# A fused attention kernel's slot loop: a third place for odd slots' tiles, logits turned group by group, no chunk steps beside tables, weights' products on quarters

## Chip, core and metric

The kernel runs on one core of a Trainium2 chip. The metric is the device time of one execution in microseconds (us). Five engines work side by side[...]: TensorE (PE), VectorE (DVE), ScalarE (ACT), GpSimd (POOL) and SyncE (SP). The last two serve here above all to issue DMA transfers.

## The reference

Everything is in fp32. The input x is 2 images of 512 channels on a 32 x 32 grid. Two layers follow each other.

Layer 0 is deformable attention with 8 heads of 64 channels. Per head, 64 key positions are found from the queries (a depthwise 6 x 6 convolution with stride 4, a gelu, a small product and a tanh), x is sampled there, and keys and values are made from the samples. A bias is added to the logits of every pair of a query (1024) and a key (64), and it is a small network of the pair's offset in position:

```
off  = tanh(gelu(dwconv(q) + b) @ off_pw) * 4             # where the keys lie
kv   = grid_sample(xn, grid + off);  k, v = kw @ kv, vw @ kv
pos  = grid_q[:, None] - grid_kv[None]                    # 1024 x 64 x 2 per head
bias = relu(signlog(pos) @ w1 + b1)                       # 128 wide
bias = relu(bias @ w2 + b2) @ w3 + b3
out  = softmax(q k^T / 8 + bias) v
x    = x + out_w @ out + out_b
x    = x + mlp(bn(x))                                     # 512 -> 2048 -> 512
```

Layer 1 is plain attention over the 1024 positions of each image with 512 channels, with a residual.

## The kernel before

**The slot loop.** 16 groups (image, pair of heads, head) of 64 keys are worked in 256 slots of 4 keys each (`NS = NG * NSL`). For the offset network a group of 16 keys, 4 slots, shares two tables `ta` and `tb` that hold the first layer's part from x and from y. Slot s does the following:

- `st_layer1` (L616): DVE adds the two tables' rows into `h1` (128 x 4096), two slots ahead.
- `st_layer2` (L633): PE multiplies h1 with the second layer's weights, 32 rows of the output at a time on four column parts of the array. The four quarters z = 0 to 3 go one after another through the three PSUM places of the pool `zp` (a tile of 128 x 1024[...]). ACT evicts each with a relu, z = 0 and 2 into tiles `rx` (L642), z = 1 and 3 into others (L644): z = 3 into `ub`, and z = 1 into `ua`, `uo`, `uc`, `uo` for s % 4 = 0 to 3. So `uo` is the tile of the odd slots. It has two places.
- `st_sum` (L652): DVE adds rx into the z = 1 tile and into ub.
- A chain of DMA transfers with addition (L654, L671, issued by POOL) and of plain copies (L678 and L687, issued by SP) folds and joins the tiles of 8 slots in SBUF until few are left. An odd slot's tile is read by a join two slots later.
- `st_layer3` (L719), every eighth slot: PE multiplies what is left with the third layer's weights into the logits `sim`, on top of the product of queries and keys (L702).

In slots with s % 4 = 0, the **table slots**, SP also loads the features for the next table (L585) and ACT makes the next `ta` and `tb` (L596, L604), after the slot's second eviction.

**Chunk steps.** The keys of later groups are made while earlier groups are worked. A generator `later()` first multiplies two weights (tile `psu`, L503), and then, for chains of one or two head pairs, runs the query product (`psq`, L273), the convolution (`prod`, L319 on ACT, reductions L334 on DVE), gelu and tanh, the features that tables are loaded from (`fe`, stored to `fdr`), the sampling (`pkv`, L471), and the products for keys (`pkk`, L485) and values (`pkv`, L487). It is cut in steps by `yield`. Every slot takes one step behind its fourth eviction until the generator is done:

```python
            if bg is not None:
                with tc.issue_after(evicted[s][1]):
                    next(bg, None)
```

**Softmax steps.** When a group's logits are whole, a second generator `softmax_steps` takes a step in slots that are no table slots, behind the second eviction. ACT brings the logits to SBUF (`ss`, L733), PE turns them by transposes into a PSUM tile `pt` of the pool `zp` (L744), ACT copies them to `sx` (L746), and maximum, exponentials, sums and scaling follow (L751 to L766). The two heads of a pair share the softmax: the first one's logits wait in `ss` until the second's are there, and both are turned together.

All PSUM tiles of the chunk and softmax steps come from the same three places of `zp` as the second layer's tiles. The order of instructions on each engine is fixed when the program is built: the source's order, changed by `issue_after`.

**After the loop** come the output projection, the MLP and layer 1, bound by PE products (L903, L956, L1087, L1185).

Of the kernel before, what the change touches and what calls it, by code (L numbers as in the profile page):

```python
# [14 lines left out]
P = 128  # L15
# [31 lines left out]
def conv_seq_kernel(ctx: ExitStack, tc: tile.TileContext, x, xt, kst, pst, cst, vec, wsm, outw, w1, w2, wl, wlt, brow, out):  # L47
# [12 lines left out]
    def col(name, i=0):  # L60
        return vs[:, VOFF[name] + i : VOFF[name] + i + 1]
# [73 lines left out]
    def flat(name):  # L135
        return zp.tile([P, 2, 512], F32, tag="ps2", name=name).rearrange("p h n -> p (h n)")
# [4 lines left out]
    with tc.tile_pool(name="lp", bufs=2) as lp:  # L141
# [273 lines left out]
        def sample(ci):  # L415
            G = CHAINS[ci]
            K = len(G)
            th = state[ci]
            gx = th[:, 0:2].rearrange("p i g j -> p (i g j)")

            nc.vector.tensor_scalar(gx, gx, 1.0, 16.0, ALU.add, ALU.mult)
            if ci > 0:
                yield


            sg = ph.tile([P, 5, 2, K * J], F32, tag="fe", name="sg")
            hat = sg[:, 0:4].rearrange("p a f j -> p (a f j)")[:, 0 : 4 * K * J]
            nc.scalar.activation(hat, gx, AF.Abs, bias=edge[:, 0:1])
            nc.scalar.activation(hat, hat, AF.Relu, bias=edge[:, 1:2])
            nc.scalar.activation(hat, hat, AF.Relu, bias=1.0, scale=-1.0)  # L430
            yield
            nc.vector.tensor_tensor(sg[:, 4], sg[:, 0], sg[:, 1], ALU.mult)
            hx = ph.tile([P, 2, K, J], F32, tag="hx", name="hx")
            hxf = hx.rearrange("p f k j -> p (f k j)")
            nc.scalar.activation(hxf, th[:, 0].rearrange("p g j -> p (g j)"), AF.Abs, bias=hb[:, 0:1])
            nc.scalar.activation(hxf, hxf, AF.Relu, bias=1.0, scale=-1.0)
            yield
            gy = th[:, 1].rearrange("p (f k) j -> p f k j", f=2)
            for i, (b, k) in enumerate(G):
                g = b * NCH + k  # L440
                xnt = ph.tile([P, 8, P], F32, name="xnt")
                nc.sync.dma_start(out=xnt, in_=xt[:, b, k])
                wk = ph.tile([P, P], F32, name="wk")
                nc.sync.dma_start(out=wk, in_=wsm[:, 512 + k * P : 512 + k * P + P])
                wt = ph.tile([P, 8, 2, J], F32, tag="xn", name="wt")
                for t in range(8):
                    if t == 4:
                        yield
                    nc.scalar.activation(wt[:, t], gy[:, :, i, :], AF.Abs, bias=hb[:, 1 + t : 2 + t])
                yield  # L450
                wtf = wt.rearrange("p t f j -> p (t f j)")
                nc.scalar.activation(wtf, wtf, AF.Relu, bias=1.0, scale=-1.0)

                kv, uv = (ph.tile([P, J], F32, name=name) for name in ("kv", "uv"))
                rowwise, natural = "p (e i t) -> p e i t", "p (i e t) -> p e i t"
                for f in range(2):
                    r, v = slice(64 * f, 64 * f + 64), sg[:, 4, f, i * J : (i + 1) * J]
                    nc.scalar.activation(
                        uv[r].rearrange(rowwise, e=2, t=16), v[r].rearrange(natural, e=2, t=16), AF.Copy,
                        scale=col("bn1b", k)[r],  # L460
                    )
                yield
                nc.vector.tensor_tensor(
                    wt, wt, hx[:, :, i, :].unsqueeze(1).to_broadcast([P, 8, 2, J]), ALU.mult
                )
                yield
                ps = flat("pkv")
                for t in range(8):
                    for f in range(2):
                        r = slice(64 * f, 64 * f + 64)  # L470
                        nc.tensor.matmul(  # L471
                            ps[r, 0:J], xnt[:, t, r], wt[:, t, f, :], start=(t == 0), stop=(t == 7)
                        )
                nc.scalar.activation(
                    kv.rearrange(rowwise, e=2, t=16), ps[:, 0:J].rearrange(natural, e=2, t=16), AF.Copy,
                    scale=bns[:, k : k + 1],
                )
                nc.vector.tensor_tensor(kv, kv, uv, ALU.add)
                if i + 1 == K and ci + 1 < len(CHAINS):
                    xn0.append(load(*CHAINS[ci + 1][0]))  # L480
                yield


                ps, pk = flat("pkv"), flat("pkk")
                nc.tensor.matmul(pk[:, 0:J], wk, kv, start=True, stop=True)  # L485
                for f_, h_, f, h in QUADS:
                    nc.tensor.matmul(  # L487
                        ps[h_, f * 512 : f * 512 + 256], kv[f_, :], uo[f_, k, h * 256 : (h + 1) * 256],
                        start=True, stop=True,
                    )  # L490
                nc.scalar.activation(kz[:, g], pk[:, 0:J], AF.Copy, scale=DH ** (-0.5))
                for f_, h_, f, h in QUADS:
                    nc.scalar.copy(vp[f_, g, h * 256 : (h + 1) * 256], ps[h_, f * 512 : f * 512 + 256])
                yield
            state[ci] = None

        def later():

            for k2 in range(2):
                ps = flat("psu")  # L500
                for k in range(2):
                    c = 2 * k2 + k
                    nc.tensor.matmul(  # L503
                        ps[:, 512 * k : 512 * k + 512], wv[:, c * P : (c + 1) * P], ow_s[:, c, :],
                        start=True, stop=True,
                    )
                nc.scalar.copy(uo[:, 2 * k2 : 2 * k2 + 2, :].rearrange("p k o -> p (k o)"), ps)
                yield
            yield from sample(0)
            for ci in range(1, len(CHAINS)):  # L510
                yield from chain(ci)
                yield from sample(ci)
# [60 lines left out]


        NS = NG * NSL
        tabs, h1s, sums, sims, logits, added = {}, {}, {}, {}, {}, {}
        evicted, raw = {}, {}


# [46 lines left out]
        def st_layer2(s):  # L626
            h1 = h1s.pop(s)
            r = []
            for z in range(4):
                ps = zp.tile([P, 2, 512], F32, name="ps2")  # L630
                for h in range(2):
                    for q in range(4):
                        nc.tensor.matmul(  # L633
                            ps[32 * q : 32 * q + 32, h, :], cw2[:, 32 * z : 32 * z + 32],
                            h1[:, 16 * h : 16 * h + 16, q, :], start=True, stop=True,
                        )
                name, bufs = (
                    ("rx", 3), (("ua", 4), ("uo", 2), ("uc", 2), ("uo", 2))[s % 4], ("rx", 3), ("ub", 3)
                )[z]
                o = lp.tile([P, 2, 512], F32, name=name, bufs=bufs)  # L640
                if z % 2 == 0:
                    nc.scalar.activation(o, ps, AF.Relu, bias=sc[:, 4 + z : 5 + z])  # L642
                else:
                    nc.scalar.activation(o, ps, AF.Relu, bias=sc[:, 4 + z : 5 + z], scale=sc[:, z : z + 1])  # L644
                r.append(o)
                if z % 2 == 1:
                    evicted.setdefault(s, []).append(nc.cur_bb.bb.instructions[-1])
            sums[s] = r
# [78 lines left out]
        def softmax_steps(gi):  # L727
            b, k, f = groups[gi]
            sim = sims.pop(gi)
            if f == 0:  # L730
                logits[0] = f_pool.tile([P, 2, 512], F32, name="ss")
            ss = logits[0]
            nc.scalar.activation(ss[:, f], sim, AF.Identity, bias=col("cb3"))  # L733
            yield

            of = [f] if gi >= NG - 2 else [0, 1][: 2 * f]
            if not of:
                return
            n = len(of)
            pt = flat("pt")  # L740
            for i, g in enumerate(of):
                for c in range(4):
                    o = 512 * i + c * P
                    nc.tensor.transpose(pt[:, o : o + P], ss[:, g, c * P : (c + 1) * P], ident)  # L744
            e = sx[:, :, of[0] : of[-1] + 1, :]
            nc.scalar.copy(  # L746
                e.rearrange("p a f j -> p f a j"), pt[:, 0 : 512 * n].rearrange("p (f a j) -> p f a j", f=n, j=J)
            )
            yield
            mx = f_pool.tile([P, 8, 2], F32, name="mx", bufs=2)  # L750
            nc.vector.tensor_reduce(mx[:, :, 0:n], e, AX.X, ALU.max)  # L751
# [36 lines left out]
        for s in range(NS):  # L788
# [18 lines left out]
                with tc.issue_after(evicted[s][0]):  # L807
                    st_tables(s // 4 + 1)
            st_sum(s, 0)
            if bg is not None:  # L810
                with tc.issue_after(evicted[s][1]):
                    next(bg, None)
            if bg is not None and state.get(len(CHAINS) - 1, 0) is None:
# [559 lines left out]
```

## Time and profile before

| | us |
|---|---|
| median of 3 runs | 2662.8 (2661.68 to 2663.64) |
| profiled execution, time | 2660.99 |
| its span, first to last instruction | 2659.2 |
| slot loop, about | 37 to 1906 |
| PE busy | 2633.2 |
| DVE busy | 2241.3 |
| ACT busy | 1687.2 |

The profile is of one execution. A line of its groups gives the source line, the engine, the operation, tiles out<-in, shapes and count, then the busy time and the mean of one in ns, and after the second bar the idle time of the engine just before, with what ended most of it. A line of the timeline gives start and length in us, the engine, the line and the tiles, and in brackets an idle time before it. A line of the waits view says who waited for whom: us in total, times, longest. A line of the windows view gives start and end, the length, and per engine the busy time with the number of its instructions. PEld is the load of weights into the array. One fp32 matmul shows as two records.

### The profile page before, as it was taken

To read this page: it belongs to the slowest core of one execution; us is meant where nothing else is said; L and a number is where in the kernel's file an instruction comes from. 1 tells how busy PE (TensorE), PEld (TensorE's weight loads), DVE (VectorE), ACT (ScalarE), POOL (GpSimd) and SP (SyncE) were. 2 spreads that over 40 slices of the span, in tenths; PEclk is the share of its full clock that TensorE was granted. 3 is DMA by queue.
4 is the path that set the end of the run, shared out by engine and by line. 5 is a ranking of instruction groups with operands and counts; after the bars stand their busy time and mean duration, and the time that the engine had idled before them with its cause. 6 is when DMAs were issued, how large, how long until landed. Compare 5 with 4: busy or idle time off the path is not lost.

```text
span 2659.2 us, 46896 instructions
## 1 busy us (share of the span) xinstructions
PE 2633.2 (99%) x19344; PEld 965.0 (36%) x19344; DVE 2241.3 (84%) x1329; ACT 1687.2 (63%) x2201; POOL 792.3 (30%) x867
## 2 busy tenths in 40 slices
PE   9999999999999999999999999999999999999999
PEld 3332322433333333233323323333334444446454
DVE  7999999999999999999999999999674483466354
ACT  5887898789978888877777777777621131114041
POOL 1333333333333333333333333333343232000000
PEclk9999999999999999999999999999999999999999
DMA  5887878888788887888888888878730111000000
GB/s 187 181 176 169 191 164 171 181 189 180 171 176 174 192 175 172 171 177 176 171 172 183 175 178 178 172 173 181 191 110 33 48 48 48 0 16 0 32 0 32
DMA packets 116293, 366.77 MB, mean 138 GB/s; under 512 B 23376, under 2 KB 27616, under 8 KB 113392
## 3 DMA queue, kind: packets, MB, share of 16 engines
q0 software_dynamic: 69408, 235.31, 46.9%
q1 hardware_dynamic: 46240, 128.15, 13.8%
q8 instruction: 153, 2.51, 0.4%
q14 instruction: 60, 0.49, 0.1%
q10 hardware_dynamic: 432, 0.31, 0.0%
HBM read 74.81 MB, written 6.55 MB: 31 GB/s over the span
## 4 chain that ended last, share of the span: by engine, by line
PE 60%; DMA 25%; DVE 7%; issue 6%; ACT 1%; POOL 1%; SPq 0%; POOLq 0%; DVEq 0%; ACTq 0%
PE ps L633 31%; PE sw L956 14%; PE sw L1087 9%; DMA uc<-uo 7%; DMA uc<-uc 6%; DMA ua<-uc 4%; DMA uc<-ub 4%; DVE h L616 3%; PE sw L1185 2%; DMA ua<-uo 1%; DVE ub L652 1%; PE psg L535 1%; DMA ua<-ua 1%; PE sim L719 1%; DVE uo L652 1%
## 5 line engine op out<-in xcount | busy, mean ns | idle before, releaser
L633 PE MATMUL ps<-h,cw 128*32 128x512 f32 x16384 | 1782.8, 592 | 8.1 <-ACT rx L642 6.1
L616 DVE CUSTOM_DVE_ANT_1 h<-ta,tb 128x4096 f32<-128x4096 f32 (+1 forms) x257 | 1131.0, 4402 | 28.1 <-PE ps L633 24.2
L633 PEld LDWEIGHTS ps<-h,cw 128*32 128x32 f32 x16384 | 554.7, 110 | 1205.0 <-issue 1114.6
L642 ACT ACTIVATE rx<-ps,sc 128x1024 f32<-128x1024 f32 x512 | 568.1, 1110 | 146.3 <-PE ps L633 116.4
L644 ACT ACTIVATE ub<-ps,sc 128x1024 f32<-128x1024 f32 x256 | 308.2, 1204 | 80.5 <-PE ps L633 80.2
L652 DVE SCALAR_TENSOR_TENSOR ub<-rx,sc,ub 128x1024 f32<-128x1024 f32 x256 | 326.8, 1277 | 6.6 <-ACT ub L644 6.6
L671 POOL DMA_DIRECT2D ua<-uc x126 | 158.3, 1272 | 299.5 <-DMA ua<-uc 292.5
L671 POOL DMA_DIRECT2D ua<-ua x189 | 225.4, 1336 | 20.2 <-DMA ua<-uo 16.2
L644 ACT ACTIVATE uo<-ps,sc 128x1024 f32<-128x1024 f32 x128 | 154.2, 1205 | 74.3 <-PE ps L633 46.2
L956 PE MATMUL sw<-xb,w1t 128*128 128x512 f32 x448 | 193.7, 592 | 2.7 <-DVE xs L123 2.7
L956 PE MATMUL sw<-hm,w2t 128*128 128x512 f32 x448 | 193.6, 592 | 0.0
L654 POOL DMA_DIRECT2D uo<-ub x127 | 126.8, 998 | 210.8 <-DVE ub L652 200.1
L652 DVE SCALAR_TENSOR_TENSOR uo<-rx,sc,uo 128x1024 f32<-128x1024 f32 x128 | 163.5, 1278 | 18.9 <-ACT uo L644 18.9
L123 DVE TENSOR_TENSOR hm<-hm,sw 128x1024 f32<-128x1024 f32 x56 | 67.6, 1218 | 104.5 <-PE sw L956 104.3
L671 POOL DMA_DIRECT2D uc<-uo x63 | 54.0, 857 | 340.8 <-DMA uc<-uo 340.4
L956 PEld LDWEIGHTS sw<-xb,w1t 128*128 128x128 f32 x448 | 85.0, 190 | 110.2 <-issue 105.7
L965 ACT ACTIVATE hm<-hm,vs 128x512 f32<-128x512 f32 x64 | 42.6, 713 | 128.4 <-DVE hm L123 128.4
L956 PEld LDWEIGHTS sw<-hm,w2t 128*128 128x128 f32 x448 | 85.1, 190 | 107.1 <-issue 106.2
L123 DVE TENSOR_TENSOR xs<-xs,sw 128x1024 f32<-128x1024 f32 (+1 forms) x48 | 55.6, 1171 | 75.9 <-PE sw L1087 36.0
L654 POOL DMA_DIRECT2D ua<-ub x64 | 59.3, 926 | 178.4 <-DVE ub L652 163.4
L1087 PE MATMUL sw<-aT,vt 128*128 128x512 f32 x224 | 96.7, 593 | 0.3 <-ACT aT L1167 0.3
L596 ACT ACTIVATE ta<-fb,vs 128x512 f32<-128x512 f32 (+1 forms) x65 | 88.5, 1364 | 10.1 <-DMA fb<-fdr 10.1
(247 smaller groups left out, 2191.6 us busy)
## 6 DMA issues: line engine op xcount, KB each, us to landing
uo<-ub POOLq DMA_DIRECT2D x127, 512.0 KB, 5.5
fb<-fdr SPq DMA_DIRECT2D x64, 512.0 KB, 5.2
ua<-ub POOLq DMA_DIRECT2D x64, 512.0 KB, 6.0
uc<-ub POOLq DMA_DIRECT2D x64, 512.0 KB, 5.0
ua<-ua POOLq DMA_DIRECT2D x63, 256.0 KB, 6.3
ua<-uo SPq DMA_DIRECT2D x63, 256.0 KB, 2.5
ua<-uo POOLq DMA_DIRECT2D x63, 256.0 KB, 5.6
uc<-uc POOLq DMA_DIRECT2D x63, 256.0 KB, 7.2
```

The costliest lines, as they stand in the source:

```text
L123: nc.vector.tensor_tensor(out, a, b_, op)
L596: nc.scalar.activation(ta.rearrange("p j x -> p x j")[:, :, j0:j1], fb[:, 0, :, j0:j1], AF.Identity, bias=col("cb1"), scale=col("w1x"),)
L616: nc.vector._custom_dve(TENSOR_ADD_SAT, out=h1[:, y : y + step].rearrange("p y t x -> p (y t x)"), in0=a.unsqueeze(1).to_broadcast([P, ste ...
L633: nc.tensor.matmul(ps[32 * q : 32 * q + 32, h, :], cw2[:, 32 * z : 32 * z + 32], h1[:, 16 * h : 16 * h + 16, q, :], start=True, stop=True,)
L642: nc.scalar.activation(o, ps, AF.Relu, bias=sc[:, 4 + z : 5 + z])
L644: nc.scalar.activation(o, ps, AF.Relu, bias=sc[:, 4 + z : 5 + z], scale=sc[:, z : z + 1])
L652: nc.vector.scalar_tensor_tensor(r[1], r[0], sc[:, z : z + 1], r[1], ALU.mult, ALU.add)
L654: nc.gpsimd.dma_start(out=sums[s][1], in_=sums[s][3], accum_op=ALU.add)
L671: nc.gpsimd.dma_start(out=out, in_=in_, accum_op=ALU.add)
L956: nc.tensor.matmul(ps[:, m, :], w[:, a, k, m * P : (m + 1) * P], x[:, b_, k, :], start=(k == 0), stop=(k == 1),)
L1087: nc.tensor.matmul(ps[:, m, :], w[:, a, k, c + m * P : c + (m + 1) * P], x[b_][:, k, :], start=(k == 0), stop=(k == nk - 1),)
L1185: nc.tensor.matmul(v[:, m, :], xbl[b_][:, k, m * P : (m + 1) * P], gn[:, a, k, :], start=(k == 0), stop=(k == 1),)
```

## The change

Five edits in the loop's generators and pools:

1. `uo` gets three places instead of two. The tile `ss` shrinks to one group's logits.
2. `softmax_steps` turns each group's logits in its own step, four transposes and a copy of 128 x 512, where a pair's eight transposes and one copy of 128 x 1024 stood in the second group's step. The last two groups were turned singly before already.
3. From slot 60 on, table slots take no chunk step.
4. The key product shares the PSUM tile of the value products (`pkk` goes into columns 256 to 319 of `pkv`).
5. The two weights' product, four matmuls of 128 x 128 by 512 in two tiles, is done on its diagonal blocks alone, as sixteen matmuls of 64 x 64 by 256 in four tiles. ACT copies each tile out in four pieces. A step still does two of the four channel blocks.

```diff
-                ps, pk = flat("pkv"), flat("pkk")
-                nc.tensor.matmul(pk[:, 0:J], wk, kv, start=True, stop=True)
+                ps = flat("pkv")
+                pk = ps[:, 256 : 256 + J]
+                nc.tensor.matmul(pk, wk, kv, start=True, stop=True)
...
-            for k2 in range(2):
+            for c in range(NCH):
                 ps = flat("psu")
-                for k in range(2):
-                    c = 2 * k2 + k
+                for f_, h_, f, h in QUADS:
                     nc.tensor.matmul(
-                        ps[:, 512 * k : 512 * k + 512], wv[:, c * P : (c + 1) * P], ow_s[:, c, :],
-                        start=True, stop=True,
-                    )
-                nc.scalar.copy(uo[:, 2 * k2 : 2 * k2 + 2, :].rearrange("p k o -> p (k o)"), ps)
-                yield
+                        ps[h_, f * 512 : f * 512 + 256], wv[f_, c * P + 64 * f : c * P + 64 * f + 64],
+                        ow_s[f_, c, h * 256 : (h + 1) * 256], start=True, stop=True,
+                    )
+                for f_, h_, f, h in QUADS:
+                    nc.scalar.copy(uo[f_, c, h * 256 : (h + 1) * 256], ps[h_, f * 512 : f * 512 + 256])
+                if c % 2 == 1:
+                    yield
...
-                    ("rx", 3), (("ua", 4), ("uo", 2), ("uc", 2), ("uo", 2))[s % 4], ("rx", 3), ("ub", 3)
+                    ("rx", 3), (("ua", 4), ("uo", 3), ("uc", 2), ("uo", 3))[s % 4], ("rx", 3), ("ub", 3)
...
-            if f == 0:
-                logits[0] = f_pool.tile([P, 2, 512], F32, name="ss")
-            ss = logits[0]
-            nc.scalar.activation(ss[:, f], sim, AF.Identity, bias=col("cb3"))
+            ss = f_pool.tile([P, 512], F32, name="ss")
+            nc.scalar.activation(ss, sim, AF.Identity, bias=col("cb3"))
             yield
+            pt = flat("pt")[:, 0:512]
+            for c in range(4):
+                nc.tensor.transpose(pt[:, c * P : (c + 1) * P], ss[:, c * P : (c + 1) * P], ident)
+            nc.scalar.copy(sx[:, :, f, :], pt.rearrange("p (a j) -> p a j", j=J))
             of = [f] if gi >= NG - 2 else [0, 1][: 2 * f]
             if not of:
                 return
             n = len(of)
-            pt = flat("pt")
-            for i, g in enumerate(of):
-                for c in range(4):
-                    o = 512 * i + c * P
-                    nc.tensor.transpose(pt[:, o : o + P], ss[:, g, c * P : (c + 1) * P], ident)
             e = sx[:, :, of[0] : of[-1] + 1, :]
-            nc.scalar.copy(
-                e.rearrange("p a f j -> p f a j"), pt[:, 0 : 512 * n].rearrange("p (f a j) -> p f a j", f=n, j=J)
-            )
...
-            if bg is not None:
+            if bg is not None and (s % 4 or s < 60):
                 with tc.issue_after(evicted[s][1]):
                     next(bg, None)
```

(The tile `uo` of the weights' product in `later()` is another one of the same name, a part of `vp`.)

More of the change, by code (lines that the diff above doesn't have):

```diff
@@ L490, in sample @@
                     )
-                nc.scalar.activation(kz[:, g], pk[:, 0:J], AF.Copy, scale=DH ** (-0.5))
+                nc.scalar.activation(kz[:, g], pk, AF.Copy, scale=DH ** (-0.5))
                 for f_, h_, f, h in QUADS:
@@ L575, in conv_seq_kernel @@
         NS = NG * NSL
-        tabs, h1s, sums, sims, logits, added = {}, {}, {}, {}, {}, {}
+        tabs, h1s, sums, sims, added = {}, {}, {}, {}, {}
         evicted, raw = {}, {}
```

## The prediction

> **What bounds the kernel now.** I read the page first. TensorE (PE) is busy for 99% of the span, and two thirds of that is one line, L633, the second layer of the bias network.
>
> ```profile
> PE 2633.2 (99%) x19344; PEld 965.0 (36%) x19344; DVE 2241.3 (84%) x1329; ACT 1687.2 (63%) x2201; POOL 792.3 (30%) x867
> L633 PE MATMUL ps<-h,cw 128*32 128x512 f32 x16384 | 1782.8, 592 | 8.1 <-ACT rx L642 6.1
> ```
>
> A slot of the loop is 64 of these records (32 matmuls, two records each), so there are 256 slots. The chain that ended last has unbroken runs of it:
>
> ```profile
> 431.73 41.25 PE ps L633 x384
> ```
>
> 384 records are 6 slots, so a slot costs 6.87 us when nothing disturbs it, and 256 cost 1759. Next the windows view, cut at the loop's start, at slot 60 (482 us, counting four evictions of L642/L644 per slot), at the end of the chunk steps (slot 155, about 1203 us), and at the loop's end:
>
> ```profile
> core 0: us, PE busy (x) PEld busy (x) DVE busy (x) ACT busy (x) POOL busy (x), PEclk, DMA share, GB/s
> 37.00:482.00 445.00, 440.56 (x4073) 134.41 (x4076) 432.22 (x231) 369.62 (x485) 149.26 (x171) 1.00 0.78 170
> 482.00:850.00 368.00, 364.37 (x3422) 125.64 (x3418) 361.32 (x187) 312.57 (x428) 131.37 (x151) 1.00 0.82 179
> 850.00:1203.00 353.00, 349.54 (x3288) 108.88 (x3284) 345.28 (x183) 299.32 (x422) 124.57 (x144) 1.00 0.81 176
> 1203.00:1700.00 497.00, 497.00 (x4620) 151.40 (x4616) 483.84 (x220) 373.16 (x420) 182.36 (x211) 1.00 0.83 177
> 1700.00:1906.00 206.00, 205.46 (x1888) 73.95 (x1880) 187.01 (x91) 155.55 (x200) 74.50 (x86) 1.00 0.81 174
> ```
>
> PE is idle for 4.4, 3.6, 3.5, 0.0 and 0.5 us: 12 us in 1869. The loop's other 100 us are PE work of its own (transposes, layer 3, the chunks' products). So no edit that removes waits can win more than these 12 us and what modelled ends hide. DVE is nearly as full as PE (97% in the first three rows). The waits view for PE over the same stretches (first two lines before slot 60, three up to 1203 us, the last after it) names who ended the idle time:
>
> ```profile
> PE ps L633 <- ACT rx L642: 2.7, 5, 1.1
> PE ps L633 <- ACT uo L644: 1.5, 1, 1.5
> PE ps L633 <- ACT rx L642: 3.4, 6, 0.9
> PE pkk L485 <- ACT rx L642: 1.6, 1, 1.6
> PE pkv L471 <- ACT uo L644: 0.7, 1, 0.7
> PE sim L719 <- DMA ua<-uc: 0.3, 1, 0.3
> ```
>
> A record lasts 592 ns while the next four start 429 ns after it, so each wait hides another 0.16 us. With that: 5.2 us before slot 60 (6 waits), 8.7 between (7.1 shown, 10 waits, with two more of 1.1 and 0.3 that are left out above), 0.8 after it (0.5 shown, 2 waits). Sum **14.7 us**.
>
> [...] eight records of the quarter products L487 take 0.66 us together and 402 ns each. [...] in this trace 32 copies of 64x256 took 367 ns each where one of 128x1024, eight times the elements, took 1005.
>
> **The change, part by part.**
>
> *Third place for uo.* No instruction is added. In odd slots ACT's second eviction waits until the DMA sums of four slots earlier have let go of the tile. Timeline of PE, ACT and POOL at slot 29:
>
> ```profile
> 258.23 4.07 PE L633 MATMUL ps<-h,cw 128*32 128x512 f32 x36 [1.46 <-ACT uo L644]
> 256.97 1.21 ACT L644 ACTIVATE uo<-ps,sc 128x1024 f32<-128x1024 f32 x1 [2.88 <-PE ps L633]
> 251.61 0.85 POOL L671 DMA_DIRECT2D ua<-uo  x1 [6.66 <-DMA ua<-uo]
> ```
>
> ACT's wait is put down to PE, which had long finished: it was the DMA of the last line, issued 5 us before. With three places the tile is due after six slots, 14 us more. Worth 1.5 + 0.16 here, and of the 0.8 after 1203 us two thirds: **-2.2 us** (0 to -2.5). Other uo waits on DMA (11.8 and 10.9 us in all) lie beside PE work and pay nothing. Queued behind that eviction were ACT's next one and DVE's sum L652; next late would be uc, which keeps two places and waited 0.6 us at most on its own DMA.
>
> *No chunk steps in table slots from slot 60.* In such a slot ACT has evictions of 2 x 1.11 + 2 x 1.20 and table fills of 1.38 + 0.68: 6.7 of 6.87 us, with nothing left for a step. 24 steps (slots 60, 64 ... 152) move on; comparing the issue orders, the 95 steps from slot 60 now end at slot 186 instead of 154. Each step moves with all it issues: ACT maps, DVE sums, PE products, and on the SP queue the loads of xn, xnt, wk, wq and the store to fdr, which pass table loads L585 and join copies L678. None is late: features of chains 3 and 4 are stored about slots 112 and 166, their tables load at 124 and 188; keys are done at 131 and 186, needed at 148 and 212. POOL's queue has no chunk instruction. No work vanishes; what can vanish is the 8.7 us of waits. They come from DVE behind its schedule (its starts are 4.33 + 1.20 + 1.20 = 6.73 us a slot, 0.13 spare) with ACT or PE waiting in order for it; so for the keys' product at 836 us:
>
> ```profile
> 835.94 0.41 PE L485 MATMUL pkk<-kv,wk 128*128 128x64 f32 x2 [1.11 <-issue]
> 835.63 0.21 DVE L478 TENSOR_TENSOR kv<-kv,uv 128x64 f32<-128x64 f32 x1
> ```
>
> PE waited for a 0.2 us sum that stood behind a 4.4 us one. Now every fourth slot lets DVE and ACT catch up, but the steps overlap the softmax steps (165 to 186 as well) longer. Bounds: all gone, -8.7; none gone, 0; more of them, the last rival. I take 55%: **-4.8 us**.
>
> *One tile for keys and values (pkk into pkv).* Same matmuls; eight PSUM places fewer to pass through. It can only spare waits for a place, 0.3 us shown in one; that lies inside the term above: **0**.
>
> *Logits group by group.* 64 transposes as before, but seven pairs in two fours:
>
> ```profile
> 1270.85 1.09 PE L744 MATMUL pt<-ident,ss 128*128 128x128 f32 x8
> 1868.66 0.66 PE L744 MATMUL pt<-ident,ss 128*128 128x128 f32 x4
> ```
>
> 2 x 0.66 - 1.09 = 0.23 more each, seven times: **+1.6 us** of PE, with nothing to hide it as PE is the bound (0.8 where a four lands in idle time, 2.5 if each waits for its PSUM place as well). ACT's copies grow from 1.0 to about 2 x 0.58 and fit.
>
> *Weights' products on quarters.* Two episodes at the loop's start, each two full matmuls, become eight quarter ones:
>
> ```profile
> 44.25 1.99 PE L503 MATMUL psu<-vp,sx 128*128 128x512 f32 x4
> 836.28 0.66 PE L487 MATMUL pkv<-vp,kv 64*64 64x256 f32 x8
> 44.85 1.20 ACT L644 ACTIVATE ub<-ps,sc 128x1024 f32<-128x1024 f32 x1
> ```
>
> By the second line two sets of quarters take about 1.1 us where 2.0 stand: 0.9 saved, twice. But ACT copies eight tiles of 0.37 (3.0 us for 1.0), and the next slot's first matmul needs the place that the eviction of the third line frees at 46.05, with PE back at 45.4 after 46.16 before: the first episode gains 0.1, the second, with no tables, 0.7. **-0.8 us** (0 to -1.8).
>
> **Sum.** -2.2 - 4.8 + 0 + 1.6 - 0.8 = **-6.2 us**. The profiled execution took 2661.0 us (span 2659.2 and 1.8 around it), 1.8 below the median of the three runs, so 2654.8 in its terms and **2656.6 us** in the median's. Head and tail of the program are not touched.
>
> **Rivals.**
> - *All waits go*: -2.5 - 8.7 + 1.6 - 1.8 = -11.4: 2651.4. For it: after slot 155, where no chunk step is left, 497 us pass without idle PE. Against: slots with steps and softmax together stay. Chance 0.20.
> - *The waits only move*: they are DVE's lag, and its work is the same; term two is 0: -2.2 + 1.6 - 0.8 = -1.4: 2661.4, no change that can be told. For it: after the skip slots the same bursts come (2.9 us reductions, features). Chance 0.28.
> - *Slower*: chunk steps now meet softmax steps in the same slots, in chain 3's features (slots 103 to 115), chain 4's reductions (143 to 157) and chain 4's keys (169 to 186), and DVE's spread and fold of the projection's blocks (about 10 us) come straight after, at 187. The one stretch of before where all met, slots 137 to 149, lost 4.3 us (waits of 1.9 and 1.6 in that window, and 5 x 0.16). Four of them are 17.2 in place of 8.7: +8.5 - 1.4 = +7.1: 2669.9. It decides from 15.4 us on, three and a half such stretches. Against: steps per slot are fewer, and reductions beside softmax in slots 77 to 90 lost nothing. Chance 0.10.
>
> **How the numbers follow.** The forecast's own case (0.42) spans 2653 to 2659. A measurement of this kernel tells about 0.2%, 5.3 us, from no change, so faster means under 2657.5: the first rival and four fifths of the forecast, 0.54; slower the last, 0.10; the rest, 0.36, within. The range leaves out half of the slower case and the low end of the first rival: 2649.5 to 2666.
>
> **What would show it.** In the profile after: PE's idle time in the loop near 5 us instead of 12; no wait on uo; 14 transpose episodes of 0.66; the psu episodes near 1.1. I am wrong if waits of L633 on rx after slot 60 keep their 3.4 us, or if new ones stand at slots 103 to 115 or 187 to 191, or if the loop's PE work itself differs by more than 2 us.

## The result and the profile after

| | before | after |
|---|---|---|
| median of 5 runs, us | 2662.8 (2660.5 to 2665.6) | 2648.8 (2648.4 to 2651.0) |
| profiled execution, us (span) | 2661.0 (2659.2) | 2648.8 (2647.0) |
| loop, first to last layer-2 matmul, us | 1866.8 | 1853.6 |
| of it TensorE (PE) busy / idle, us | 1854.8 / 12.1 | 1848.4 / 5.3 |

The ratio after/before is 0.9953 (95% interval 0.9943 to 0.9964): 12.5 us faster, twice the forecast of 6.2; the medians differ by 14.0. The median lies 0.7 us under the low end of the range; the ratio times the median of before, 2650.3, lies just inside it. All of it is in the loop (-13.2 us in the profiled executions; what follows the loop took 755.2 and 756.1).

The new lines are L635 for layer 2 (L633 before), L644 and L646 for its evictions (L642 and L644), L721 for layer 3 (L719), L486 and L488 for keys and values (L485 and L487), L738 for the logits' transposes (L744). First the page, the lines of busy time and of layer 2:

```profile
PE 2628.8 (99%) x19368; PEld 953.9 (36%) x19368; DVE 2240.1 (85%) x1329; ACT 1693.2 (64%) x2222; POOL 791.0 (30%) x867
L635 PE MATMUL ps<-h,cw 128*32 128x512 f32 x16384 | 1776.4, 592 | 5.2 <-ACT rx L644 4.0
```

The share is still 99%, with 24 instructions more; yet layer 2's busy time is 6.4 us less for the same 16384 records. The windows view at the same cuts as before:

```profile
core 0: us, PE busy (x) PEld busy (x) DVE busy (x) ACT busy (x) POOL busy (x), PEclk, DMA share, GB/s
37.00:482.00 445.00, 441.21 (x4133) 133.52 (x4136) 435.71 (x232) 376.39 (x504) 150.84 (x173) 1.00 0.79 171
482.00:850.00 368.00, 368.00 (x3448) 119.53 (x3444) 360.93 (x181) 309.13 (x410) 131.46 (x152) 1.00 0.83 181
850.00:1203.00 353.00, 352.13 (x3301) 107.93 (x3296) 345.40 (x172) 297.92 (x405) 128.49 (x148) 1.00 0.83 179
1203.00:1700.00 497.00, 496.40 (x4652) 152.53 (x4648) 489.01 (x242) 386.25 (x466) 180.41 (x207) 1.00 0.82 176
1700.00:1893.00 193.00, 193.00 (x1780) 68.91 (x1772) 176.25 (x85) 146.85 (x193) 70.56 (x81) 1.00 0.82 175
```

PE's idle time between 482 and 1203 us is 0.9 us, where it was 7.1. In the first window it has fallen little, and yet PE runs 60 records more in the same 445 us, of which only 24 are the quarters' (32 records of L503 for 8): there the time came from somewhere that shows no wait. What is left in the waits view (two lines from before 482 us, one up to 1203, one after it; us in total, times, longest):

```profile
PE ps L635 <- ACT rx L644: 2.7, 4, 1.3
PE ps L635 <- ACT ub L646: 0.7, 2, 0.4
PE ps L635 <- ACT rx L644: 0.8, 1, 0.8
PE ps L635 <- ACT rx L644: 0.6, 1, 0.6
```

No wait on `uo` and none of the keys' products is left. So the two terms on waits came about. (New are the waits on `ub`, at slots 1 and 2 behind the weights' products, and those on `rx` at slots 114 and 160.) But idle time fell by 6.8 us only, and PE's busy time fell by 6.4 although the fours of transposes had been added. The prediction had named "if the loop's PE work itself differs by more than 2 us" as a sign of error.

The timeline of one keys' step (a chunk step that makes keys and values) shows what changed. Some words for it: four matmuls of layer 2 or 3, one for each column part, mostly start within 0.02 us of each other (so do 3888 of layer 2's 4062 sets of four records in the trace after), and the next four 0.43 us later. Such 0.43 us are called a *turn* here, four layer-3 matmuls that belong together a *quartet*, and a quartet whose four do not stand together in TensorE's order is *torn*. At slot 9, before:

```profile
111.37 0.43 PE L485 MATMUL pkk<-kv,wk 128*128 128x64 f32 x2
...
111.51 1.20 ACT L644 ACTIVATE ub<-ps,sc 128x1024 f32<-128x1024 f32 x1 [0.60 <-PE ps L633]
...
111.74 0.66 PE L487 MATMUL pkv<-vp,kv 64*64 64x256 f32 x8
...
112.33 0.62 PE L719 MATMUL sim<-ua,w3f 128*32 128x512 f32 x1
...
112.78 0.62 PE L633 MATMUL ps<-h,cw 128*32 128x512 f32 x2
112.78 0.59 PE L719 MATMUL sim<-ua,w3f 128*32 128x512 f32 x1
```

and after:

```profile
110.82 0.43 PE L486 MATMUL pkv<-kv,wk 128*128 128x64 f32 x2
...
110.95 1.21 ACT L646 ACTIVATE ub<-ps,sc 128x1024 f32<-128x1024 f32 x1 [0.60 <-PE ps L635]
...
111.18 0.66 PE L488 MATMUL pkv<-vp,kv 64*64 64x256 f32 x8
...
111.77 1.49 PE L635 MATMUL ps<-h,cw 128*32 128x512 f32 x12
```

After it, layer 2 goes on 0.59 us after the values' products began. Before, a *lone* matmul of layer 3, one of the four of a quartet, has PE for itself from 112.33 to 112.78 (its first record; two records make one matmul, in layer 2 16384 for 8192), and layer 2 starts only when the eviction of `ub` has ended at 112.71. The other three of that quartet came some three slots later, at 134.96. Seven of the kernel's eight keys' steps before were followed by such a lone matmul (six of layer 3, one of the keys' products for `sim`); none is in the changed kernel. Two causes were possible, and they were the subject of the experiments: the *order* (torn quartets), and a *place* in PSUM (`flat` takes its tiles from the same ring of three places as layer 2's `ps2`, so two tiles for keys and values make layer 2 wait for the eviction just begun).

### The profile page after: what moved, and what is told of

The parts are those of the page before. It is cut to its first block, busy times and chain, and to the rows that moved or that the text cites. A ratio compares the mean times of both kernels' runs of the same rounds, so it can differ in the third digit from the quotient of the medians.

```text
span 2647.0 us, 46958 instructions
## 1 busy us (share of the span) xinstructions
PE 2628.8 (99%) x19368; PEld 953.9 (36%) x19368; DVE 2240.1 (85%) x1329; ACT 1693.2 (64%) x2222; POOL 791.0 (30%) x867
## 4 chain that ended last, share of the span: by engine, by line
PE 92%; DVE 3%; issue 2%; ACT 2%; DMA 1%; DVEq 0%; POOL 0%; SPq 0%; ACTq 0%; POOLq 0%
PE ps L635 62%; PE sw L953 15%; PE sw L1084 9%; PE sw L1182 2%; PE sim L721 1%; PE psg L537 1%; DVE h L618 1%; PE sw L900 1%; DVE ub L654 0%; DMA wr<-in_wlt 0%; PE pkv L471 0%; DVE xs L908 0%; PE sim L704 0%; PE pt L738 0%; DMA uc<-uo 0%
## 5 line engine op out<-in xcount | busy, mean ns | idle before, releaser
L635 PE MATMUL ps<-h,cw 128*32 128x512 f32 x16384 | 1776.4, 592 | 5.2 <-ACT rx L644 4.0
L635 PEld LDWEIGHTS ps<-h,cw 128*32 128x32 f32 x16384 | 543.0, 110 | 1203.1 <-issue 1131.4
L644 ACT ACTIVATE rx<-ps,sc 128x1024 f32<-128x1024 f32 x512 | 567.9, 1109 | 145.1 <-PE ps L635 127.1
L646 ACT ACTIVATE ub<-ps,sc 128x1024 f32<-128x1024 f32 x256 | 308.2, 1204 | 93.6 <-PE ps L635 93.5
L673 POOL DMA_DIRECT2D ua<-ua x189 | 225.9, 1372 | 16.8 <-DMA ua<-uo 11.9
L646 ACT ACTIVATE uo<-ps,sc 128x1024 f32<-128x1024 f32 x128 | 154.2, 1204 | 53.0 <-PE ps L635 52.7
L987 ACT COPY hm<-sw 128x1024 f32<-128x1024 f32 x8 | 8.1, 1010 | 136.3 <-PE sw L953 136.3
```

Of the source, the lines that this page charges most:

```text
L635: nc.tensor.matmul(ps[32 * q : 32 * q + 32, h, :], cw2[:, 32 * z : 32 * z + 32], h1[:, 16 * h : 16 * h + 16, q, :], start=True, stop=True,)
L673: nc.gpsimd.dma_start(out=out, in_=in_, accum_op=ALU.add)
```

## The experiments

Medians are set against the kernel before, run on the same chip beside it. A ratio's interval is about ±0.1%, ±3 us, so sizes below that are read from the traces, slot by slot. Of the changed kernel's variants only *without one tile* has an interval clear of the changed kernel's own. A stretch of slots is the time from the last eviction of one slot to the last of a later one. Where nothing was changed it mostly repeats to 0.02 us between executions.

| kernel | median, us | ratio to before | 95% interval |
|---|---|---|---|
| the changed kernel | 2648.8 | 0.9953 | 0.9943 to 0.9964 |
| one tile alone | 2657.5 | 0.9980 | 0.9972 to 0.9987 |
| order alone | 2660.9 | 0.9992 | 0.9984 to 1.0000 |
| skip alone | 2659.3 | 0.9987 | 0.9980 to 0.9994 |
| logits alone | 2665.8 | 1.0014 | 1.0007 to 1.0020 |
| changed, torn 1 + 3 | 2648.2 | 0.9951 | 0.9939 to 0.9964 |
| changed, torn 2 + 2 | 2650.6 | 0.9960 | 0.9947 to 0.9972 |
| changed, without one tile | 2654.6 | 0.9977 | 0.9967 to 0.9988 |
| changed, without the skip | 2653.1 | 0.9972 | 0.9963 to 0.9981 |
| changed, two tiles, its order kept | 2651.8 | 0.9963 | 0.9951 to 0.9976 |
| changed, without the third `uo` | 2652.2 | 0.9962 | 0.9950 to 0.9975 |
| changed, torn far apart | 2653.3 | 0.9969 | 0.9957 to 0.9980 |
| changed, without the fours | 2649.3 | 0.9954 | 0.9941 to 0.9968 |

**One tile alone**, on the kernel before.

```diff
-                ps, pk = flat("pkv"), flat("pkk")
+                ps = flat("pkv")
+                pk = ps[:, 256 : 256 + J]
...
```

> The kernel before with one part of the change: keys and values of a chunk in one PSUM tile. Theory A (order): what the tile changes is the order in which the builder lays out TensorE's instructions; six layer-3 quartets that stand as 1 + 3, one to three slots apart, and one quartet of keys' products (also 1 + 3) become whole, and a quartet that is torn costs about 0.8 us (slots 8 to 15 took 60.09 us before and 59.26 after): 6 to 7 times 0.8, so -5 us (-4 to -6), with the same waits as before. Rival B (places): it only spares waits for a PSUM place, 0.3 us shown: 0 to -1 us. My prediction's term was 0.

Measured 0.9980: -5.3 us, the size that theory A gave, where the prediction had 0. The size alone doesn't prove its cause, as the next run shows. In its trace PE's busy time in the loop fell from 1854.8 to 1851.6 us. Slots 8 to 17 took 73.02 us for 73.84, slots 32 to 41 77.89 for 78.73, slots 114 to 125 89.84 for 90.68: 0.82 to 0.84 less at each. The waits between 482 and 1203 us stayed, now at L634 and L486:

```profile
PE ps L634 <- ACT rx L643: 3.7, 5, 0.9
PE pkv L486 <- ACT rx L643: 2.6, 2, 1.6
```

Its profiled execution (2660.9) was itself among its slowest. The reason is a wait at slot 28 that has nothing to do with the tile:

```profile
251.09 1.28 ACT L597 ACTIVATE ta<-fb,vs 128x512 f32<-128x512 f32 x1 [4.11 <-DMA fb<-fdr]
...
253.91 2.15 PE L634 MATMUL ps<-h,cw 128*32 128x512 f32 x11 [3.23 <-ACT rx L643]
```

The table was loaded late, ScalarE stood, and the eviction behind the fill came late. Before and after show no such wait at that slot. It is one of the few that come and go from execution to execution.

**Order alone**, on the kernel before: both tiles stay.

```diff
+            with tc.issue_after(last[0]):        # last[0]: the slot's last layer-2 matmul
                 for m in range(len(parts[1])):
...
+                with tc.issue_after(last[0]):
                     for f_, h_, o, h in QUADS:
...
```

> The kernel before with its two PSUM tiles for keys and values kept, and nothing else changed but TensorE's order: the matmuls of layer 3 and of the keys' products are tied to come after the slot's last layer-2 matmul, so that all seven torn quartets are whole, in the very order that the one tile gives. Theory A (order): the same as with one tile, -5 us (-4 to -6). Rival B (places): 0, since no place is added or taken.

Measured 0.9992: -2.1 us, its interval from -4.3 to 0. Neither theory: less than half of what the one tile gave, though TensorE's order was the same. Both causes had to be at work, which the later runs confirm. Slot by slot this trace is 0.36 to 0.54 us shorter than that of before at slots 10, 35, 73, 114 and 155, 2.1 us in all. Those are the five torn quartets that have a product of another shape between their pieces; at the other two (slots 67 to 69 and 107 to 109) it is the same within 0.04 us.

**Skip alone**, on the kernel before.

```diff
-            if bg is not None:
+            if bg is not None and (s % 4 or s < 60):
```

> The kernel before with one part of the change: no chunk step in table slots from slot 60. Theory A: it takes away the waits of TensorE between 482 and 1203 us, 8.7 us of them, of which most (5 to 8) go, and one torn quartet fewer than before (0.8): -6 us (-5 to -8). Rival B (the waits only move, and the changed kernel's gain is all from order): -1 us. My prediction's term was -4.8.

Measured 0.9987: -3.5 us (-5.3 to -1.6), between the two. PE's idle time in the loop fell from 12.1 to 6.9 us, which is the forecast's mechanism and size; its waits from 482 to 1203 us are down to these:

```profile
PE ps L633 <- ACT rx L642: 1.3, 2, 1.0
PE ps L633 <- ACT ub L644: 0.4, 1, 0.4
```

PE's busy time rose by 0.9 us, and the lone matmuls, still seven, stand at other slots.

**Logits alone**, on the kernel before.

```diff
+            pt = flat("pt")[:, 0:512]
+            for c in range(4):
+                nc.tensor.transpose(pt[:, c * P : (c + 1) * P], ss[:, c * P : (c + 1) * P], ident)
+            nc.scalar.copy(sx[:, :, f, :], pt.rearrange("p (a j) -> p a j", j=J))
...
```

> The kernel before with one part of the change: logits turned group by group. Theory A: seven pairs of transposes in two fours each, 0.23 us more for a pair by the prediction, 0.27 by the changed kernel's trace (ten and a half against 8.4 us in all): +1.6 to +1.9 us. Rival B: some fours land where TensorE idles anyway, +0.8. Rival C: each four waits for its place too, +2.5 to +3.

Measured 1.0014: +3.7 us (+1.9 to +5.3), at the upper end. In its trace the first group's four costs 0.72 to 0.75 us in each of its seven slots, and the second's saves 0.13 to 0.45 where eight stood before: 2.5 us in all. On top, at slot 95, stands a wait of 0.74 us of layer 2 on `ub` that before hasn't got. There is also one wait of 2.45 us on `uo` at slot 105, of a kind that no trace with three places has. So the work of the fours was forecast too small by all, and one four in fourteen shows a wait, not each as rival C had it.

**Torn 1 + 3**, on the changed kernel.

```diff
+            n = 1 if i == 0 else len(quad)       # quad: the quartet's four matmuls
+            for p_, k_ in quad[:n]:
+                nc.tensor.matmul(*p_, **k_)
+            rest.extend(quad[n:])                # issued at the end of the next slot
...
```

> The changed kernel with 16 of its layer-3 quartets (the first of every group) torn on purpose: one matmul where the four stand now, the other three one slot later; nothing else on TensorE moves. Theory A (order): each torn quartet takes two turns of TensorE (2 x 429 ns each for the two passes) in place of one, so 0.83 to 0.86 us more, 16 times: +13 to +14 us against the changed kernel (2648.8), so about 2662. Rival (the torn quartets of before cost nothing, the 7 us are from elsewhere): 0, so 2649.

Measured 0.9951, as the changed kernel: no cost, and theory A in its simple form is dead. The stretches of 16 slots, each with one torn quartet, differ from the changed kernel's by -0.55 to +0.35 us, with a sum of -0.1. The timeline of one of them:

```profile
133.74 0.59 PE L729 MATMUL sim<-ua,w3f 128*32 128x512 f32 x1
133.75 0.63 PE L635 MATMUL ps<-h,cw 128*32 128x512 f32 x3
134.17 0.59 PE L729 MATMUL sim<-ua,w3f 128*32 128x512 f32 x1
...
140.64 0.60 PE L809 MATMUL sim<-ua,w3f 128*32 128x512 f32 x3
141.04 0.59 PE L635 MATMUL ps<-h,cw 128*32 128x512 f32 x1
141.07 0.61 PE L809 MATMUL sim<-ua,w3f 128*32 128x512 f32 x3
```

The lone matmul shares its turns at 133.74 and 134.17 with three records of layer 2 each. The 60 records from 134.20 on start in 16 turns: by the count three in the first, four in each of fourteen, and one in the last, beside the three of the quartet at 140.64. So by this count every turn is full, though the quartet is torn.

**Torn 2 + 2**, the same with `n = 2`.

> The same 16 quartets of the changed kernel torn into 2 + 2, one slot apart. Theory A, if a torn quartet simply takes a second turn however it is torn: +13 to +14 us as with 1 + 3. Theory A'[...]: clearly less than with 1 + 3, some +7. Rival (order costs nothing): 0.

Measured 0.9960, +1.8 us by the medians (the ratios' intervals overlap). In the trace 14 of the 16 stretches lie within 0.35 us of the changed kernel's; one of +3.05 holds a wait of 2.04 us at slot 28, again behind a table fill that waited for its load; one of +1.04 stays unexplained. So tearing costs nothing in this way either.

**Changed, without one tile** (`ps, pk = flat("pkv"), flat("pkk")` again).

> The changed kernel with two PSUM tiles for keys and values as before, all other parts kept. TensorE's order then has five torn quartets again. Theory A (order): 5 x 0.86 = +4.3 us (+3.5 to +6) against the changed kernel, about 2653. Theory B (the gain of one tile was run scatter or places): 0 to +1, about 2649.5.

Measured 0.9977 against 0.9953, 6.4 us slower: it is the largest part of the change. Seven torn quartets were in this kernel, not the five expected (five of layer 3, two of the keys' products for `sim`). Where the time went follows two runs below.

**Changed, without the skip** (`if bg is not None:` again).

> The changed kernel with the chunk steps back in table slots, all other parts kept. If the parts simply add up, it loses what the skip alone gained on the kernel before: +3 us, about 2652. If whole quartets free TensorE time that becomes waits on ScalarE and VectorE unless the skip is there too (with one tile alone, TensorE's stalls in the loop rose by some 3.6 us in the trace while its own work fell by 7): +6 to +9 us, about 2656, with waits of layer 2 on rx and of the keys' products between 482 and 1203 us.

Measured 0.9972, 5.1 us slower, between the two. The loop is 4.4 us longer, and all of it is idle: PE busy 1848.4 us as in the changed kernel, idle 9.6 for 5.3. One wait among them is the 0.74 us on `ub` at slot 95 that *logits alone* has too. It shows in no other kernel; only these two have both the fours and chunk steps in table slots after slot 60. The waits from 482 to 1203 us are back:

```profile
PE ps L635 <- ACT rx L644: 1.7, 5, 0.5
PE pkv L486 <- ACT rx L644: 1.7, 1, 1.7
PE pkv L486 <- ACT ub L646: 1.5, 1, 1.5
```

**Changed, two tiles, its order kept**: without one tile, but with the ties of *order alone*.

> The changed kernel with two PSUM tiles for keys and values as before, but with the matmuls of layer 3 and of the keys' products tied behind the slot's last layer-2 matmul, so that TensorE's order is that of the changed kernel to the instruction. Theory A (one tile pays only by the order): as the changed kernel, 2649 (0 to +1 against it). Rival B (the merged tile pays by its places in PSUM): as all but one tile, 2654.6 (+5 to +6).

Measured 0.9963: 2.7 us slower than the changed kernel (4.0 us in the loop of its trace), between A and B once more. The keys' step of slot 9 in its trace:

```profile
110.86 0.43 PE L485 MATMUL pkk<-kv,wk 128*128 128x64 f32 x2
...
110.99 1.21 ACT L646 ACTIVATE ub<-ps,sc 128x1024 f32<-128x1024 f32 x1 [0.60 <-PE ps L634]
...
111.22 0.66 PE L487 MATMUL pkv<-vp,kv 64*64 64x256 f32 x8
...
112.25 1.49 PE L634 MATMUL ps<-h,cw 128*32 128x512 f32 x12 [0.37 <-ACT ub L646]
```

With the lone matmul gone, the wait that it had covered stands in the open: 0.37 us shown on the eviction of `ub`, which frees the place that the second tile has taken. The same 0.35 to 0.37 stands at all eight keys' steps. What these two kernels add to the changed kernel in the stretches with a keys' step (us; "between" is a product of another shape, a feature product or a transpose, between the pieces of the torn quartet):

| slots | without one tile (torn) | two tiles, order kept | between |
|---|---|---|---|
| 8 to 17 | 0.82 | 0.47 | yes |
| 32 to 41 | 0.88 | 0.73 | yes |
| 68 to 73 | 0.44 | 0.56 | not torn here |
| 74 to 80 | 2.11 | 0.26 | yes, twice |
| 122 to 129 | 0.44 | 0.44 | no |
| 130 to 133 | 0.43 | 0.44 | no |
| 178 to 186 | 0.83 | 0.44 | no |
| 187 to 191 | 0.97 | 0.44 | yes |
| sum | 6.9 | 3.8 | |

The second column is the price of the place: in the slot behind the step itself it is 0.42 to 0.44 in all eight, 3.5 us, and what the rows have beside that lies in other slots. The first adds what the tears cost on top: 0.40 to 0.54 in the slot at five steps, 2.2 us, and nothing in the two rows from 122 to 133. Another 1.4 us of the row of 74 to 80 stand at slot 77, ahead of the lone matmul, with a wait of 0.88 for a DMA; nothing shows that they belong to the tile. The row of 178 to 186 has 0.39 more though only layer 2 lies between the pieces; its torn quartet is that of the keys' products for `sim`, on quarters of 64, a shape of its own. That this is why is argued, not tried.

**Torn far apart**: *torn 1 + 3*, with the three issued three slots later, not one.

```diff
-                while rest:
+                while rest and s >= late[0]:     # late[0]: three slots after the lone one
```

> The changed kernel with 16 layer-3 quartets torn into 1 + 3 with three slots between in place of one. Between the pieces of seven of them (done about slots 64, 80, 96, 128, 160, 192, 224) stands a product of another shape, a transpose or a keys' product; between those of the other nine there is layer 2 alone. Theory A'' (torn costs only where a product of another shape[...] stands between the pieces): the seven cost 0.43 to 0.86 each, the nine nothing: +3 to +6 us against the changed kernel, and slot by slot in the trace exactly there. Rival A' (distance or number of slots out of step counts): the sixteen alike. Rival C (only a lone matmul right behind a product of another shape costs): 0.

Measured 0.9969: +4.3 us against the changed kernel. Slot by slot it is theory A'': slots 64 to 67 +0.85, 74 to 80 +0.28, 90 to 97 +0.83, 122 to 129 +0.83, 157 to 163 +0.90, 192 and 193 +0.85, 222 to 227 +0.83, and nowhere else more than +0.07 (at slot 114 a wait of 0.77 is missing). In the single slots in which the three come, the seven cost 0.84 to 0.94, 6.1 us in all; the row of 74 to 80 shows less since the changed kernel's own trace is 0.56 us slower at slot 77. The nine cost nothing. The timeline of the first:

```profile
484.05 0.59 PE L729 MATMUL sim<-ua,w3f 128*32 128x512 f32 x1
484.06 0.63 PE L635 MATMUL ps<-h,cw 128*32 128x512 f32 x3
484.48 0.59 PE L729 MATMUL sim<-ua,w3f 128*32 128x512 f32 x1
484.51 14.29 PE L635 MATMUL ps<-h,cw 128*32 128x512 f32 x125
498.74 0.66 PE L745 MATMUL pt<-ident,ss 128*128 128x128 f32 x4
```

Here the lone matmul shares its turns as before, and the cost stands ahead of the transposes (128*128 where layer 2 is 128*32). The 125 records of layer 2 start in 33 turns: by the count three in the first, four in each of 30, and the last two, at 497.78 and 498.21, alone in theirs, 2 x 0.43 us. The transposes start at 498.74. Why the two stand alone is not shown: a record doesn't name its column part.

**Changed, without the third `uo`** (`("uo", 2)` twice).

> The changed kernel with two places for uo again, all other parts kept; each engine's order is that of the changed kernel to the instruction. Theory A: the waits on uo of the profiled execution of before, 1.5 us at slot 29 and 0.8 later with what ends hide: +2 us, 2651. Theory B: these waits fall anew in every execution (one tile alone showed 3.2 us in slots 18 to 31 where order alone showed none, logits alone 2.7 in slots 104 to 113), and the profiled execution of before was a mild one: +3 to +5 us, 2652 to 2654, and a wider scatter than the changed kernel's 2.6 us.

Measured 0.9962, 2.4 us slower (3.5 by the medians alone, 2.9 in the loop of its trace): between theory A and theory B, and the runs spread over 4.9 us, wider than the changed kernel's 2.6, as B said. The waits views of PE and of ACT in the loop:

```profile
PE ps L635 <- ACT uo L646: 1.7, 2, 0.9
...
ACT uo L646 <- DMA uc<-uo: 16.1, 11, 3.5
ACT uo L646 <- DMA ua<-uo: 14.3, 10, 2.7
```

PE's waits are at slots 19 and 161, where before had one at 29 and the order alone one of 1.8 us at 197: they fall elsewhere in most executions (*skip alone* repeats the one at slot 29). The 3.2 us that the expectation put down to `uo` was the late table shown above. With three places ACT shows no wait on `uo` for a DMA at all.

**Changed, without the fours.**

```diff
+            if f == 0:
+                logits[0] = sx.rearrange("p a f j -> p (a f j)")[:, 0:512]
+            else:
+                logits[1] = f_pool.tile([P, 512], F32, name="ss")
...
```

> A version meant to beat both: the changed kernel with the logits turned in pairs as before, so seven pairs of eight transposes and not two fours. The place that the third uo tile needs is had in another way: the first group's logits wait in the flat first half of the softmax's own tile, only the second's have a tile (2 KB a partition less than before). Theory A: it gains what the fours cost, 7 x 0.27 = 1.9 us: about 2647. Rival: the first group's logits wait for the softmax before, which holds the tile, and put the eviction behind it on ScalarE: 0 to +2 us.

Measured 0.9954, and 2649.3 us: the same as the changed kernel. In its trace the loop is 1.9 us shorter (1851.7), as theory A summed up. Slot by slot it is 0.72 to 0.75 less where the first group's four stood and 0.12 to 0.46 more where eight stand for the second's four: 2.6 us less in all, and other slots take the rest back. The medians don't show it; so no version is shown to beat the changed kernel.

## Why the prediction was right and wrong

**Direction and four of five terms were right.** *Third place*: -2.2 forecast, -2.4 by leaving it out. The mechanism held, but the size came from one execution's waits, which mostly fall elsewhere in the next, so luck has a part in it. ("Two thirds" of the 0.8 after 1203 us was misread: the wait on `uo` there is 0.18 of the 0.5 shown, two fifths with the 0.16 us that the prediction adds to each wait.) *Skip*: -4.8 forecast, -5.1 by leaving it out but -3.5 on the kernel before, in idle time as said. The share of 55% was a guess, so here too the closeness is luck in part. That VectorE's lag was what these waits came from was argued, and was not tried by itself. *Weights' products on quarters*: -0.8 forecast; slots 0 to 7 take 0.58 us less than in *one tile alone*, nearly all in the second episode, as the prediction had it; the new waits on `ub`, 0.43 and 0.30 us, take part of the gain back. *Logits*: +1.6 forecast, too little: 2.5 and 2.6 us by the slots of *logits alone* and of the version without the fours. The groups view of the loop, of after and then of before, has the transposes at 1.5 us more, and the weights' products after:

```profile
L738 PE MATMUL pt<-ident,ss 128*128 128x128 f32 x60 | 9.8, 287 | 0.0
...
L503 PE MATMUL psu<-vp,sx 64*64 64x256 f32 x32 | 2.4, 395 | 0.1
```

```profile
L744 PE MATMUL pt<-ident,ss 128*128 128x128 f32 x60 | 8.3, 280 | 0.0
```

**The step that failed** is "*One tile for keys and values* ... It can only spare waits for a place, 0.3 us shown in one; that lies inside the term above: 0". It was worth 6.4 us by the ratios; 5.7 of them are found in the traces, 3.5 for the place and 2.2 for torn quartets. Two readings went wrong in it:

- The waits view was taken as the list of all waits for a place. In the kernel before, the place was waited for at six of the eight steps (not at slots 107 and 148), but a lone matmul ran meanwhile (112.33 to 112.78 at slot 9), so PE counted as busy. With no lone matmul there, in *two tiles, its order kept*, it costs 0.44 us at each of eight. The ceiling of 12 us of idle time, and the rival *all waits go* that was built on it (2651.4), missed this for the same reason: the result lies below them although 5.3 us of idle time are left.
- "Same matmuls" was taken for the same work. Where a product of another shape comes between a lone matmul and the other three, six of the seven stretches of *torn far apart* take 0.83 to 0.90 us more, and in the timeline of the first, two records of layer 2 have a turn each to themselves. That is on top of the place in part only: where the lone one stands in the wait for the place, both together cost 0.82 to 0.97, as the table shows.

With the measured terms, -2.4 - 5.1 - 6.4 + 2.6 - 0.6 = -11.9 us, against -12.5 measured. Each of the first three carries some ±4 us, so the match is closer than it could be asked to be. On the kernel before, the one tile and the skip gave less (5.3 and 3.5) than they cost when left out of the changed kernel (6.4 and 5.1); the intervals don't decide whether that is an interaction.

**What the rivals missed.** *The waits only move* said new waits would replace the old in later slots: between 1203 and 1893 us PE waits 0.6 us. The *slower* rival's stretches, slots 103 to 115 and 187 to 191, have one wait of 0.8 us, at slot 114.

**What stays open:** what the 1.4 us at slot 77 of *without one tile* come from, whether VectorE's lag is the root of the waits that the skip takes away, and why the version without the fours is 1.9 us shorter in the loop of one trace and not in the medians.

## What to carry to other kernels

Busy is not full: where four matmuls of an engine share a turn, look for records that have a turn alone, since a wait for a place can hide behind one (here at 112.33 before, for 0.45 us), and then no view of idle time has it. An edit that changes no instruction can change the order that the builder makes (here none of seven lone matmuls is left); compare the orders, and keep groups that share a turn together, above all where an instruction of another shape follows (here 0.83 to 0.90 us in six of seven tears). A small tile drawn from the ring of a busy stage costs that stage a place (here 0.42 to 0.44 us at each of eight steps).

## What the runs showed of the hardware

In *torn 1 + 3* three records of layer 2 start at 133.75, before the second record of the lone matmul, at 134.17, though that matmul was issued ahead of them. The sixteen tears of that kernel change its stretches by -0.1 us in all. In *torn far apart* the nine with layer 2 alone between the pieces cost nothing (no other stretch has more than +0.07 us), and the seven with a product of another shape between them, transposes or keys' products, cost 0.84 to 0.94 us each in the single slots in which the three come.

Stretches of the loop that two kernels share mostly repeat to 0.02 us: slots 246 to 255 all take the same within 0.01 us in the traces of before and after. The spread of several us between the profiled executions comes from a few waits behind DMAs, such as the table load ahead of slot 28 (0 to 3.2 us of idle PE), and from what follows the loop (754.0 to 758.2 us, in kernels that share that part).
